# Column directions' input projections: u read in row order, PSUM written with steps

## The chip, the core and the metric

The kernel runs on one core of a Trainium2 chip, whose engines work side by side from queues of their own: TensorE (PE in the profile), VectorE (DVE), ScalarE (ACT), GpSimd (POOL) and the DMA queues, most of them issued by SyncE (SP). The time is the device time of one execution in microseconds (us), as the median of several executions. All data is fp32.

## What is computed

The reference is a network of two layers on a batch of 4 images with 384 channels and 32 x 32 positions (L = 1024). The first layer is a selective scan in four directions and a mixture of experts; the second is attention and an MLP. The change lies in the scan:

```
x0 = x.reshape(B, D, H * W)                              # row order
x1 = transpose(x, (0, 1, 3, 2)).reshape(B, D, H * W)     # column order
xs = stack([x0, x1, x0[..., ::-1], x1[..., ::-1]], 1)    # k = 0, 1, 2, 3
x_dbl = einsum('bkdl,kcd->bkcl', xs, x_proj_weight)      # 12 + 16 + 16 = 44 rows
dts, Bs, Cs = x_dbl[:, :, :12], x_dbl[:, :, 12:28], x_dbl[:, :, 28:]
dt = softplus(einsum('bkrl,kdr->bkdl', dts, dt_projs_weight) + bias)
h[l] = h[l-1] * exp(dt[l] * A) + dt[l] * u[l] * Bs[l]    # 16 states a channel
y[l] = sum over states of h[l] * Cs[l]
```

Directions 1 and 3 walk the image by columns. The einsum that makes x_dbl treats each position by itself, so its result does not depend on the order in which positions are taken, as long as each lands in its place.

## The kernel before

**Units.** `scan_layer` cuts the scan into 32 units: 4 batches, 4 directions in the order 0, 1, 3, 2, and 2 halves of 512 positions each. Directions 1 and 3 are called column units here (16 of the 32), 0 and 2 row units. u, the normalised input of a batch, stays in SBUF as 128 partitions x 3 chunks of channels x 1024 positions in row order: position (h, w) is element 32 h + w.

**Projection.** `project` (from L292) runs one unit ahead. It makes xd, 44 rows by 512 positions, with three matmuls into one PSUM bank, one for each chunk of channels (L316 to L319). `part(c)` (L302) gives the moving operand: for a row unit 512 contiguous elements of u, for a column unit the pattern "w, then h", in which neighbours lie 32 elements apart. `split` (L307) gives the bank in the shape w by h, which for a column unit is the contiguous bank in column order. ACT copies xd to SBUF (L321). Its B and C rows go to DRAM (L323) and come back, broadcast, as the tiles bcs (L329). The rest of xd is multiplied by the weights of dt (L344). ACT makes a softplus of it; DVE multiplies dt by u for the tile du (L382), with `part(c)` and `split` again; and both go to DRAM (L384, L385).

**Scan.** `chunk` (from L388) handles 128 channels of a unit. It reads dt and dt*u back (L403). For every group of states POOL multiplies dt*u by B into a tile bx (L419, 2 x 512 elements), ACT makes da = exp(dt*A) (L428), DVE scans along the positions (L433), and the product with C is made by DVE (L440) or POOL (L447). PE adds the states up with a selection matrix, into acc (L454). A bx tile is one of six (`bufs=6`): it is free when its acc matmuls are done. DVE adds acc into y (L281, L285). For a column unit it reads acc in PSUM with a step of 32 elements, so that y stays in row order.

**Order of the work.** A scheduler places all instructions at build time; each engine then takes its own in that fixed order. `next(project)` in `scan_layer` sets the xd block at the start of the unit before. From batch 1 on the tail of the batch before (`tail_batch`: routing, experts L906 to L925, attention L1030 to L1076, the last layers) is laid into the scan, and its matmuls stand in the same PE queue. After the last unit only tail work is left.

Of the kernel before, what the change touches and what calls it, by code (L numbers as in the profile page):

```python
# [20 lines left out]
DC = D // P  # L21
HW = 32
# [8 lines left out]
XD = R + 2 * NS  # L31
# [77 lines left out]
def halves(i):  # L109
    return slice(i * HF, (i + 1) * HF)  # L110


class Body:
# [68 lines left out]
    def scan_layer(self, x1, between):  # L182

        nc, tc, a = self.nc, self.tc, self.a
        with ExitStack() as ctx:
# [67 lines left out]
            for n, unit in enumerate(units):  # L253
# [3 lines left out]
                if n + 1 < len(units):  # L257
                    nb = units[n + 1][0]
                    if nb not in us:
                        us[nb] = start(nb)  # L260
                    project = self.project(units[n + 1], us[nb], wx, work, dram, psum, ahead)
                    next(project)
# [4 lines left out]
                for c in range(DC):  # L267
                    acc = psum.tile([P, HF], F32, tag="ps", name="acc")
                    for _ in self.chunk(
                        unit, n % NH == 0, c, fed, carry, nega, sel, acc, work, dap  # L270
                    ):
                        next(project, None)
                    if k % 2 == 0:
                        ys = y[:, c, halves(i)]
                        out = acc
                    else:
                        w = slice(i * (HW // NH), (i + 1) * (HW // NH))
                        ys = y[:, c, :].rearrange("p (h w) -> p h w", h=HW)[:, :, w]
                        out = acc.rearrange("p (w h) -> p h w", h=HW)
                    if k == 0:  # L280
                        nc.vector.scalar_tensor_tensor(  # L281
                            ys, us[b][:, c, halves(i)], dsum[:, c : c + 1], out, op0=ALU.mult, op1=ALU.add
                        )
                    else:
                        nc.vector.tensor_add(ys, ys, out)  # L285
# [6 lines left out]
    def project(self, unit, u, wx, work, dram, psum, made):  # L292

        nc, a = self.nc, self.a
        b, k, i = unit
        by_cols = k % 2 == 1
        w = slice(i * (HW // NH), (i + 1) * (HW // NH))  # L300

        def part(c):  # L302
            if by_cols:
                return u[:, c, :].rearrange("p (h w) -> p w h", h=HW)[:, w, :]
            return u[:, c, halves(i)]

        def split(ap):  # L307
            return ap.rearrange("p (w h) -> p w h", h=HW) if by_cols else ap

        def k2(name, shape=(P, HF)):  # L310
            return work.tile([*shape], F32, tag="k2", name=name, bufs=6)

        wdt = k2("wdt", (R, D))
        nc.sync.dma_start(out=wdt, in_=a["wdt"][:, k, :])
        ps = psum.tile([P, HF], F32, tag="ps", name="xd_ps")
        for c in range(DC):  # L316
            nc.tensor.matmul(
                split(ps[:XD, :]), wx[:, c, k, :], part(c), start=(c == 0), stop=(c == DC - 1)
            )  # L319
        xd = k2("xd", (XD, HF))  # L320
        nc.scalar.copy(xd, ps[:XD, :])  # L321
        rows = dram.tile([2 * NS, HF], F32, tag="rows", name="rows")
        nc.sync.dma_start(out=rows, in_=xd[R:XD, :])  # L323
        view = rows.rearrange("(t g n) l -> n t g l", t=2, g=NG)
        bcs = []
        for g in range(NG):
            bc = work.tile([P, 2, HF], F32, tag="bcs", name="bcs", bufs=5)
            for n in range(NJ):
                nc.sync.dma_start(  # L329
                    out=bc[n * DB : (n + 1) * DB], in_=view[n, :, g].partition_broadcast(DB)  # L330
                )
            bcs.append(bc)

        dd = dram.tile([2, D, HF], F32, tag="dd", name="dd")
        made += [bcs, dd]
        yield  # L340

        def begin(c):
            ps = psum.tile([P, HF], F32, tag="ps", name="dt_ps")
            nc.tensor.matmul(ps, wdt[:, c * P : (c + 1) * P], xd[:R, :], start=True, stop=True)  # L344
            bias = self.col("dtb", k * DC + c)
            mag, one_e, lnw = k2("mag"), k2("one_e"), k2("lnw")
            relu = k2("relu") if b == 0 else ps
            nc.scalar.activation(mag, ps, AF.Abs, bias=bias)
            nc.scalar.activation(relu, ps, AF.Relu, bias=bias)
            nc.scalar.activation(mag, mag, AF.Exp, scale=-1.0)  # L350
            nc.scalar.activation(one_e, mag, AF.Identity, bias=1.0)
            nc.scalar.activation(lnw, one_e, AF.Ln)
            if b == 0:
                nc.scalar.activation(one_e, one_e, AF.Identity, bias=1.0, scale=-1.0)
                terms = [lnw, one_e, mag, relu]
                for t in terms:
                    nc.tensor.matmul(
                        ps, self.ident, t, start=(t is terms[0]), stop=(t is terms[-1])
                    )
            else:  # L360
                nc.scalar.activation(one_e, one_e, AF.Identity, bias=self.minus1)
            return ps, mag, one_e, lnw

        def behind(engine):
            if self.place_behind is None:
                return nullcontext()
            return self.tc.issue_after(self.place_behind[engine])

        for c in range(DC):
            ps, mag, one_e, lnw = begin(c)  # L370
            yield
            if b > 0:
                with behind("pool"):
                    nc.gpsimd.tensor_sub(mag, one_e, mag)
                    nc.gpsimd.tensor_sub(lnw, lnw, mag)
            yield
            d, du = mag, one_e
            rows = slice(c * P, (c + 1) * P)
            with behind("dve"):
                if b > 0:  # L380
                    nc.vector.tensor_add(ps, ps, lnw)
                nc.vector.tensor_mul(split(du), split(ps), part(c))  # L382
            nc.scalar.copy(d, ps)  # L383
            nc.sync.dma_start(out=dd[0, rows, :], in_=d)  # L384
            ins = nc.sync.dma_start(out=dd[1, rows, :], in_=du).ins  # L385
        made.append(ins)
# [602 lines left out]
    def attention(self, xc, sums, room):  # L989
# [68 lines left out]

        steps = [(t, i, j) for t in range(HEADS // 2) for i in range(NH) for j in range(MB)]
        made = [project(0)]  # L1060
        ahead = scores(0, made[0][0], 0, 0, None)
        atts = []
# [366 lines left out]
```

## Time and profile before

| what | us |
|---|---|
| median of 3 executions | 4361.97 |
| lowest and highest | 4361.64 and 4367.63 |
| the profiled execution | 4365.25 |
| its span, first to last instruction | 4363.5 |
| of the span: PE busy | 3382.3 |
| POOL busy | 3049.6 |
| DVE busy | 2919.3 |
| ACT busy | 2504.0 |

The profile is of one execution. Its page gives busy sums, the span in 40 slices of 109 us (a digit is the busy share in tenths, PEclk the clock that TensorE was granted, in tenths of full speed), and groups of equal instructions with count, busy time, mean length, and the idle time of the engine ahead of them with what ended most of it. Other views of the trace are used too: one source line's instructions, busy sums in windows of time, and the timeline, in which neighbours of one kind are merged. Matmuls overlap: the next one starts before the one before has ended, so what a matmul costs PE is the distance of two starts and not its length.

### The profile page before, as it was taken

Reading aid. Unit: us, or ns where it says so; the run is one execution under the profiler, and the core shown is the slowest. Engines: PE = TensorE matmul, PEld = TensorE weight load, DVE = VectorE, ACT = ScalarE, POOL = GpSimd, SP = SyncE. Lnnn points to the kernel's source line nnn. Section 1 sums busy time; section 2 is a strip of 40 time slices with the busy share of each in tenths; the row PEclk is TensorE's granted clock in tenths of the full one; section 3 lists DMA queues with packets and bytes.
Section 4 is the critical chain, followed back from the end, with each engine's and each line's share of the span. In section 5 each row is a group of like instructions: output and inputs, shape, how many; then the busy total and the mean of one; then the engine's idle time right before and its main releaser. Section 6 shows DMA issues by size and latency. Waiting matters only on the chain. (4 is left out here: it accounts for less than half of the span.)

```text
span 4363.5 us, 46084 instructions
## 1 busy us (share of the span) xinstructions
PE 3382.3 (78%) x13436; PEld 1581.3 (36%) x13436; DVE 2919.3 (67%) x4331; ACT 2504.0 (57%) x4470; POOL 3049.6 (70%) x1475
## 2 busy tenths in 40 slices
PE   6545544379997895579997888579998799999896
PEld 2111111145553221235554322135554234666323
DVE  5888888967877868968787867968887740200102
ACT  4445545556665875466575777466666564343353
POOL 5999998898988968688898978789898831000100
PEclk7766776589997997779998999679999899999997
DMA  5444354577886534457779534457789434336200
GB/s 136 114 122 116 106 162 115 151 228 214 231 241 183 142 109 139 125 174 213 213 229 279 154 95 132 115 158 225 215 233 273 134 108 142 116 126 214 63 17 15
DMA packets 404756, 684.74 MB, mean 157 GB/s; under 512 B 50960, under 2 KB 206480, under 8 KB 404496
## 3 DMA queue, kind: packets, MB, share of 16 engines
q1 hardware_dynamic: 395184, 655.37, 51.9%
q0 software_dynamic: 8192, 25.17, 1.7%
q8 instruction: 108, 1.77, 0.2%
q14 instruction: 152, 1.25, 0.1%
q10 hardware_dynamic: 1120, 1.18, 0.1%
HBM read 561.47 MB, written 120.06 MB: 156 GB/s over the span
## 5 line engine op out<-in xcount | busy, mean ns | idle before, releaser
L419 POOL TENSOR_TENSOR bx<-dtr,bcs 128x1024 f32<-128x1024 f32 x768 | 1792.4, 2361 | 229.6 <-PE acc L454 118.7
L428 ACT ACTIVATE da<-dtr,nega 128x512 f32<-128x512 f32 x1536 | 1045.3, 690 | 945.8 <-DVE bx L440 564.3
L447 POOL TENSOR_TENSOR bx<-bx,bcs 128x1024 f32<-128x1024 f32 x384 | 903.1, 2359 | 179.1 <-DVE carry L444 74.3
L906 PE MATMUL h_ps<-xc,w 128*128 128x256 f32 (+1 forms) x3168 | 675.0, 368 | 60.8 <-DMA w<-in_w 18.7
L454 PE MATMUL acc<-bx,sel 128*32 128x512 f32 x3072 | 496.8, 697 | 289.2 <-POOL bx L447 232.4
L921 PE MATMUL y_ps<-w,hs 128*128 128x384 f32 x1824 | 643.2, 505 | 38.1 <-ACT hs L914 37.8
L906 PEld LDWEIGHTS h_ps<-xc,w 128*128 128x128 f32 x3168 | 556.1, 200 | 238.7 <-issue 112.8
L433 DVE TENSOR_TENSOR_SCAN bx<-da,carry,bx 128x512 f32<-128x512 f32 x384 | 474.7, 1270 | 129.3 <-ACT da L428 65.8
L433 DVE TENSOR_TENSOR_SCAN bx<-da,bx 128x512 f32<-128x512 f32 x384 | 453.3, 1210 | 117.1 <-POOL bx L419 59.2
L433 DVE TENSOR_TENSOR_SCAN da<-da,carry,bx 128x512 f32<-128x512 f32 x384 | 478.0, 1274 | 66.5 <-ACT da L428 60.9
L440 DVE TENSOR_TENSOR bx<-da,bcs 128x512 f32<-128x512 f32 x768 | 510.3, 680 | 3.7
L433 DVE TENSOR_TENSOR_SCAN da<-da,bx 128x512 f32<-128x512 f32 x384 | 456.2, 1219 | 63.3 <-ACT da L428 53.0
L921 PEld LDWEIGHTS y_ps<-w,hs 128*128 128x128 f32 x1824 | 350.0, 196 | 325.8 <-issue 78.2
L1036 ACT ACTIVATE ex<-s_ps 128x512 f32<-128x512 f32 x512 | 300.8, 592 | 156.6 <-PE s_ps L1030 154.4
L1030 PE MATMUL s_ps<-w 64*128 64x512 f32 x1024 | 307.9, 662 | 53.1 <-ACT ex L1036 51.8
L911 ACT ACTIVATE hs<-h_ps,bb 128x256 f32<-128x256 f32 (+1 forms) x528 | 201.0, 441 | 218.8 <-PE h_ps L906 218.4
L1076 PE MATMUL o_acc<-ex,vt 128*64 128x512 f32 x1024 | 287.0, 638 | 18.1 <-ACT ex L1036 11.5
L454 PEld LDWEIGHTS acc<-bx,sel 128*32 128x32 f32 x3072 | 80.0, 116 | 585.9 <-POOL bx L447 319.8
L942 POOL TENSOR_TENSOR diag<-ident,g_weight 128x1024 f32<-128x1024 f32 x8 | 15.0, 1893 | 345.6 <-PE xc_ps L889 331.0
L925 DVE TENSOR_TENSOR y<-y_ps,bb 128x384 f32<-128x384 f32 x76 | 41.7, 549 | 273.4 <-PE y_ps L921 273.4
L344 PE MATMUL dt_ps<-xd,wdt 12*128 12x512 f32 x192 | 123.2, 726 | 71.4 <-ACT mag L383 43.8
L1030 PEld LDWEIGHTS s_ps<-w 64*128 64x128 f32 x1024 | 82.8, 190 | 256.0 <-ACT ex L1036 206.0
(214 smaller groups left out, 3767.2 us busy)
## 6 DMA issues: line engine op xcount, KB each, us to landing
w<-in_w SPq DMA_DIRECT2D x352, 576.0 KB
dtr<-dd SPq DMA_DIRECT2D x1536, 128.0 KB
bcs<-rows SPq DMA_DIRECT2D x512, 128.0 KB
dd<-one_e SPq DMA_DIRECT2D x96, 256.0 KB
dd<-mag SPq DMA_DIRECT2D x96, 256.0 KB
rows<-zero SPq DMA_DIRECT2D x76, 192.0 KB
xs<-rows SPq DMA_DIRECT2D x32, 384.0 KB
made<-y SPq DMA_DIRECT2D x32, 384.0 KB
```

What stands on the lines that cost most here:

```text
L419: pool = nc.gpsimd.tensor_mul(bx, dtr[q][1], bc[:, 0].unsqueeze(1).to_broadcast([P, 2, HF])).ins
L428: nc.scalar.activation(da, dtr[q][0][:, j, :], AF.Exp, scale=nega[:, col : col + 1])
L433: nc.vector.tensor_tensor_scan(run(h), run(da), run(bx[:, j, :]), 0.0 if first else hold, ALU.mult, ALU.add,)
L440: dve = nc.vector.tensor_mul(bx[:, j, :], h, cg).ins
L447: pool = nc.gpsimd.tensor_mul(bx, bx, cg.unsqueeze(1).to_broadcast([P, 2, HF])).ins
L454: nc.tensor.matmul(acc[lo : lo + DB, :], sel, out[q][:, j, :], start=(g == 0), stop=(g == NG - 1),)
L906: nc.tensor.matmul(ps[:, r, :], w1[(f + r) // wf][:, c, (f + r) % wf * P : ((f + r) % wf + 1) * P], xc[:, c, :], start=(c == 0), stop=(c = ...
L911: nc.scalar.activation(hs[:, f + r, :], ps[:, r, :], AF.Identity, bias=bb[:, f + r : f + r + 1])
L921: nc.tensor.matmul(out[:, :D], hs[:, f, t * P : (t + 1) * P], w2[f // wf][:, f % wf, :], start=(f == 0), stop=(f == FC - 1),)
L1030: ins = nc.tensor.matmul(ps, w[rows, j * P : (j + 1) * P], w[rows, halves(i)], start=True, stop=True).ins
L1036: done.append(nc.scalar.activation(ex[:, o, :], ps, AF.Exp, scale=HD**-0.5, accum_out=sums[:, t, 2 * j + o, i : i + 1],).ins)
L1076: ins = nc.tensor.matmul(out[cols, :], made[t][1][:, j, cols], ex[:, o, :], start=(j == 0), stop=(j == MB - 1),).ins
```

## The change

For a column unit, the three xd matmuls read u in row order: for each of the 32 rows h, the 16 contiguous elements that belong to this half of the columns. The result is still kept in column order, so the PSUM side takes the steps: the bank is written in the shape h by w, where neighbours (w, w+1) lie 32 elements apart. Row units keep their patterns. L382 keeps `part` and `split`. The shapes and the sums stay; only the order in which a matmul takes its 512 positions changes. Eight lines are added, so line numbers after this place are 8 higher in the changed kernel: the matmul of L317 is L325 there.

```
--- before.py
+++ after.py
@@ -299,6 +299,14 @@
         by_cols = k % 2 == 1
         w = slice(i * (HW // NH), (i + 1) * (HW // NH))
 
+        def rows_of(c):
+            if by_cols:
+                return u[:, c, :].rearrange("p (h w) -> p h w", h=HW)[:, :, w]
+            return u[:, c, halves(i)]
+
+        def to_rows(ap):
+            return ap.rearrange("p (w h) -> p h w", h=HW) if by_cols else ap
+
         def part(c):
             if by_cols:
                 return u[:, c, :].rearrange("p (h w) -> p w h", h=HW)[:, w, :]
@@ -315,7 +323,7 @@
         ps = psum.tile([P, HF], F32, tag="ps", name="xd_ps")
         for c in range(DC):
             nc.tensor.matmul(
-                split(ps[:XD, :]), wx[:, c, k, :], part(c), start=(c == 0), stop=(c == DC - 1)
+                to_rows(ps[:XD, :]), wx[:, c, k, :], rows_of(c), start=(c == 0), stop=(c == DC - 1)
             )
         xd = k2("xd", (XD, HF))
         nc.scalar.copy(xd, ps[:XD, :])
```

More of the change, by code (lines that the diff above doesn't have):

```diff
@@ L300, in project, with rows_of, to_rows @@
         w = slice(i * (HW // NH), (i + 1) * (HW // NH))
+        def rows_of(c):
+            if by_cols:
+                return u[:, c, :].rearrange("p (h w) -> p h w", h=HW)[:, :, w]
+            return u[:, c, halves(i)]
+        def to_rows(ap):
+            return ap.rearrange("p (w h) -> p h w", h=HW) if by_cols else ap
         def part(c):
@@ L317, in project @@
             nc.tensor.matmul(
-                split(ps[:XD, :]), wx[:, c, k, :], part(c), start=(c == 0), stop=(c == DC - 1)
+                to_rows(ps[:XD, :]), wx[:, c, k, :], rows_of(c), start=(c == 0), stop=(c == DC - 1)
             )
```

## The prediction

> **What bounds the kernel now.** I read the page's busy sums and 40 slices first, then the costliest groups.
>
> ```profile
> PE 3382.3 (78%) x13436; PEld 1581.3 (36%) x13436; DVE 2919.3 (67%) x4331; ACT 2504.0 (57%) x4470; POOL 3049.6 (70%) x1475
> PE   6545544379997895579997888579998799999896
> POOL 5999998898988968688898978789898831000100
> PEclk7766776589997997779998999679999899999997
> ...
> L419 POOL TENSOR_TENSOR bx<-dtr,bcs 128x1024 f32<-128x1024 f32 x768 | 1792.4, 2361 | 229.6 <-PE acc L454 118.7
> ```
>
> POOL leads the scan (31 slices): a unit needs 24 products of L419 and 12 of L447, 36 x 2.36 = 85.0 us, and a unit of batch 0 lasts 88 us (118 to 206 us). In batches 1 to 3 the expert, attention and MLP matmuls of the batch before share PE with the scan, and the windows by unit show PE as full as POOL:
>
> ```profile
> 206.00:294.00 88.00, 47.86 (x135) 11.24 (x134) 78.76 (x115) 44.87 (x70) 83.50 (x37) 0.69 0.44 115
> 1120.00:1231.00 111.00, 105.94 (x425) 61.94 (x424) 90.00 (x102) 68.32 (x108) 98.31 (x46) 0.97 0.76 213
> ```
>
> (Columns: window, its length, busy PE, weight load, DVE, ACT, POOL, clock, DMA.) In batch 0 a shorter PE job buys nothing; in the second window PE idles 5 us of 111.
>
> Next the changed line alone. An fp32 matmul leaves two records, so a unit's three leave six.
>
> ```profile
> L317 PE MATMUL xd_ps<-u,wx x6: 1034/1035/1035, 1029.0 to 1033.2; 128*44 128x512 f32 x6
> ...
> L317 PE MATMUL xd_ps<-u,wx x6: 592/592/627, 1586.0 to 1588.2; 128*44 128x512 f32 x6
> ...
> L317 PE MATMUL xd_ps<-u,wx x6: 593/1061/1082, 789.2 to 793.5; 128*44 128x512 f32 x6
> ```
>
> First a column unit, then a row unit at full clock, then a row unit mostly at half clock. A record's length holds its latency; what it costs PE is the spacing of starts: (1033.2-1029.0)/5 = 0.84 us for columns, (1588.2-1586.0)/5 = 0.44 at full clock; at 0.1 us resolution. From the block's busy time, finer: (5.33-1.035)/5 = 0.859 us, and, with 2.77 us in the windows below, (2.77-0.592)/5 = 0.436, or 0.429 past the first start. So I use 858 and 429 ns: 512 columns at 1.68 and 0.84 ns. The column price stays near 858 at any clock; a contiguous record costs about 854 at half clock (1061-593 = 468 more, latency included).
>
> Last, one block in the timeline, with who stands behind it:
>
> ```profile
> 1120.23 5.33 PE L317 MATMUL xd_ps<-u,wx 128*44 128x512 f32 x6
> 1125.60 0.58 ACT L321 COPY xd<-xd_ps 44x512 f32<-44x512 f32 x1 [3.11 <-PE xd_ps L317]
> 1128.92 1.06 PE L454 MATMUL acc<-bx,sel 128*32 128x512 f32 x8
> 1130.07 4.67 POOL L419 TENSOR_TENSOR bx<-dtr,bcs 128x1024 f32<-128x1024 f32 x2 [3.19 <-PE acc L454]
> ```
>
> PE runs the block in its order, so the acc matmuls come later, their bx buffers come free later, and POOL stands 3.19 us. ACT stands too, with da (L428) behind the copy.
>
> [...] No matmul of before writes with steps, so this is untested, and it is the crux. [...]
>
> **The change part by part.** The instruction lists of the two programs are the same on every engine in number, order and waits, DMAs included; nothing is moved. Only the 16 column units' xd matmuls differ, 96 records.
>
> *Removed:* the stepped read. The new read takes runs of 16 fp32, 64 bytes[...]; I cost it as contiguous. Up to 858-429 = 429 ns a record at full clock, 2.57 us a unit; nothing at half clock. The granted clock in these windows (columns: window, length, PE, weight load, clock, DMA) sorts the units:
>
> ```profile
> 1028.90:1034.30 5.40, 5.33 (x6) 0.70 (x6) 1.00 0.59 225
> ...
> 1836.50:1842.00 5.50, 5.36 (x6) 0.92 (x6) 0.56 0.03 7
> ...
> 2746.60:2752.00 5.40, 5.36 (x6) 0.92 (x6) 0.50 0.28 100
> ...
> 3189.90:3192.80 2.90, 2.77 (x6) 0.64 (x6) 1.00 1.04 282
> ```
>
> The last is a row unit. Of the 12 column units of batches 1 to 3, ten stand at 1.00; the two at 0.56 and 0.50 do not, and I count them at nothing. PE saves 10 x 2.57 = 25.7 us there.
>
> *Added:* PSUM writes at a step of 32 fp32, three passes accumulating. Bounds: 0.84 ns a column (free), 1.68 (as SBUF), 3.35 (twice that). The nearest rows are DVE's, on the same two steps:
>
> ```profile
> L382 DVE TENSOR_TENSOR one_e<-dt_ps,u x3: 989/1001/1028, 256.7 to 290.2; 128x512 f32<-128x512 f32 x3
> L285 DVE TENSOR_TENSOR y<-y,acc x2: 665/676/687, 269.2 to 292.4; 128x512 f32<-128x512 f32 x2
> ...
> L382 DVE TENSOR_TENSOR one_e<-dt_ps,u x3: 677/681/691, 605.3 to 638.9; 128x512 f32<-128x512 f32 x3
> L285 DVE TENSOR_TENSOR y<-y,acc x3: 678/689/689, 577.4 to 639.5; 128x512 f32<-128x512 f32 x3
> ```
>
> The first pair is a column unit, the second a row unit. Reading u with steps costs DVE 320 ns; reading acc in PSUM at the very step the change writes costs nothing[...]. [...] I take free. It is a read, not an accumulating write: hence the two rivals.
>
> *How much reaches the end.* In batch 0 the four blocks lie beside POOL's products (83.5 of 88 us busy), which start at their own pace from full buffers; I take 0. Were that cover gone, the three blocks there at a clock of 0.92 to 1.00 would give 3 x 2.57 = 7.7 us. ACT's copy of xd and the DMAs of rows and bcs behind it come up to 2.57 us earlier, for a unit that starts 88 us or more later: 0. In batches 1 to 3 I count POOL's stalls right behind each block, capped by what the block gives up (2.57, or 1.72 where an acc group sits after the fourth record). By start time: 913.0: 1.50; 1120.2: 2.57 (stall 3.19); 1231.1: 1.72 (1.79); 1953.4: 1.26; 2067.2: 2.57 (2.85); 2884.3: 2.50; 3102.6: 1.05; at 1029.0, 2156.6 and 2976.2 none. The stalls at 913.0, 1231.1 and 2884.3 stand as "issue", but POOL starts just as an acc group ends. Sum 13.2 us, half of PE's 25.7. Some will be lost (late next: DVE's scans, for which POOL waits at L447), some gained where PE is short and POOL does not show it; I leave 13.2.
>
> The profiled execution took 4365.25 us (span 4363.5, 1.75 around it): 4352.1. It lay 3.3 above the median of 4361.97, so the forecast is 4361.97-13.2 = **4349**.
>
> **Rivals.**
> 1. *PSUM's step costs what SBUF's did*, 1.68 ns a column: records stay at 858, time **4362**. For: [...]SBUF's behaviour. Against: L285.
> 2. *Slower: the accumulating write needs over 1.68 ns[...].* The place is the same block; it decides from 858 ns a record. At 1287 PE gains 12 x 2.57 = 31 us, half reaches POOL: 4378. At 1717 it is 62 us, some 42 reach POOL as buffers run dry, and in batch 0 ACT, which already stands 2.7 to 3.7 us at three of the four blocks, delays DVE (79 of 88 us busy) by some 2 us each: +50, **4412**. [...] Against: L285 again, and reads and writes of contiguous sums that keep pace at 429.
> 3. *Writes are free but the time is given back*: POOL's next stall, on DVE or a DMA, swallows it. In 913 to 1325 us POOL waits 19 us for DVE, 14 for DMA and 12 for PE. Some 4 us are left: **4358**.
>
> **How the numbers follow.** Forecast 0.44, rival 1 0.18, rival 2 0.24, rival 3 0.14. The likeliest case alone spans 4336 (all of 25.7) to 4353. The range, 4336 to 4380, takes in rivals 1 and 3 and the mild end of 2, leaving out some 0.18: 0.03 under 4336, and 0.15 of rival 2 from a record of about 1350 ns on. About 0.2% (8.7 us) is what a measurement here can tell from no change: faster 0.44, same 0.33 (rivals 1 and 3, less 0.01, and 0.02 of rival 2's weakest form), slower 0.23.
>
> **What would show it.** Free: column records of L325 at 592 ns at full clock, blocks of 2.77 us instead of 5.33, POOL's stall at the block near 1120 us under 1 us. Rival 1: records at 1035. Rival 2: over 1035. Rival 3: 592, and POOL idle moved from PE to DVE or DMA. I am wrong if the run-lengths of 16 cost reads of their own, or if the time moves though the records do not.

## The result and the profile after

The changed kernel takes 4345.85 us (median of 8 executions) against 4362.18 us (8 executions of the kernel before): ratio 0.9962, interval 0.9951 to 0.9973, or 16.6 us less (11.8 to 21.4). The forecast was 4349, 13.2 us less. The profiled execution took 4349.06 us, with a span of 4347.3.

The page's busy sums and slices after the change:

```profile
PE 3336.8 (77%) x13436; PEld 1575.1 (36%) x13436; DVE 2919.5 (67%) x4331; ACT 2504.3 (58%) x4470; POOL 3049.9 (70%) x1475
...
PE   6545544379997884579897887579997899998896
...
POOL 5999998898989978689898978789888830000100
PEclk8666666589998997789998998779999899999997
...
L427 POOL TENSOR_TENSOR bx<-dtr,bcs 128x1024 f32<-128x1024 f32 x768 | 1793.5, 2364 | 217.0 <-PE acc L462 116.0
```

PE's busy time fell by 45.5 us; the other engines' stayed within 0.4. So the change took work from PE alone; the other engines do the same work and only wait less. Of the 45.5 us, the 16 column blocks themselves give about 35 (from 85.9 to 51.0, the time under at least one record of L317 or L325). The rest is about what two executions of one kernel differ by: a second trace of the kernel before has 3373.0 us of PE, 9.3 less than the first.

The changed line itself, in the column unit shown before (now at 1019.9 us) and in a row unit:

```profile
L325 PE MATMUL xd_ps<-u,wx x6: 592/592/627, 1019.9 to 1022.1; 128*44 128x512 f32 x6
...
L325 PE MATMUL xd_ps<-u,wx x6: 593/593/627, 2612.1 to 2614.2; 128*44 128x512 f32 x6
```

They are the same, 592 and 593 ns a record at the median: the stepped PSUM write costs a column unit nothing that can be seen here. Windows on the same line (columns: window, length, PE, weight load, clock, DMA share, GB/s) show the block near 1111 us and the two at a low clock:

```profile
1110.90:1113.80 2.90, 2.77 (x6) 0.64 (x6) 1.00 1.05 226
1820.00:1826.00 6.00, 5.11 (x6) 1.01 (x6) 0.57 0.12 32
2726.00:2731.00 5.00, 4.23 (x6) 0.93 (x6) 0.63 0.30 108
```

2.77 us as forecast; in the window at a clock of 0.57 the block still takes 5.11 us, in the one at 0.63 it takes 4.23. Both took 5.36 before.

The timeline at the block near 1111 us:

```profile
1110.96 2.77 PE L325 MATMUL xd_ps<-u,wx 128*44 128x512 f32 x6
...
1113.77 0.58 ACT L329 COPY xd<-xd_ps 44x512 f32<-44x512 f32 x1 [0.56 <-PE xd_ps L325]
...
1117.10 1.06 PE L462 MATMUL acc<-bx,sel 128*32 128x512 f32 x8
...
1118.24 6.99 POOL L427 TENSOR_TENSOR bx<-dtr,bcs 128x1024 f32<-128x1024 f32 x3 [0.62 <-PE acc L462]
```

ACT's wait for xd went from 3.11 us to 0.56, POOL's wait for acc from 3.19 to 0.62. The latter is the full 2.57 us that this block was to give.

POOL's waits in a stretch where PE is nearly full, from the first product of unit 9 to that of unit 13 (the same work in both; 904.7 to 1331.6 us before, 898.6 to 1315.4 after; columns: us in total, times, longest). Before:

```profile
POOL bx L447 <- DVE carry L444: 11.8, 6, 4.3
POOL bx L419 <- PE acc L454: 11.7, 5, 4.8
POOL bx L419 <- DMA dtr<-dd: 11.4, 4, 5.4
...
POOL bx L419 <- issue: 3.3, 2, 1.8
...
```

After:

```profile
POOL bx L455 <- DVE carry L452: 12.4, 5, 4.3
...
POOL bx L427 <- DMA dtr<-dd: 7.5, 2, 5.1
POOL bx L427 <- PE acc L462: 6.6, 4, 3.4
POOL bx L427 <- issue: 2.7, 1, 2.7
...
```

The wait for acc fell by 5.1 us and "issue" (idle time for which the profile shows no wait) by 0.6, which are the stalls that the forecast had counted here (1.50, 2.57 and 1.72). The wait for a DMA fell by 3.9, which it had not counted. That is scatter: a second trace of the kernel before has 8.0 us of it in this stretch, 3.4 less than the first, without any change. The waits for DVE did not fall.

### The profile page after: what moved, and what is told of

It is laid out like the page before. It is cut to its first block, busy times and chain, and to the rows that moved or that the text cites. A ratio compares the mean times of both kernels' runs of the same rounds, so it can differ in the third digit from the quotient of the medians.

```text
span 4347.3 us, 46084 instructions
## 1 busy us (share of the span) xinstructions
PE 3336.8 (77%) x13436; PEld 1575.1 (36%) x13436; DVE 2919.5 (67%) x4331; ACT 2504.3 (58%) x4470; POOL 3049.9 (70%) x1475
## 3 DMA queue, kind: packets, MB, share of 16 engines
q8 instruction: 108, 1.77, 0.2%
## 5 line engine op out<-in xcount | busy, mean ns | idle before, releaser
L1084 PE MATMUL o_acc<-ex,vt 128*64 128x512 f32 x1024 | 283.3, 630 | 19.1 <-ACT ex L1044 11.8
L933 DVE TENSOR_TENSOR y<-y_ps,bb 128x384 f32<-128x384 f32 x76 | 41.6, 548 | 264.3 <-PE y_ps L929 264.2
```

The costliest lines, as they stand in the source:

```text
L1084: ins = nc.tensor.matmul(out[cols, :], made[t][1][:, j, cols], ex[:, o, :], start=(j == 0), stop=(j == MB - 1),).ins
```

## The experiments

Where the gain arises is read from one mark, the start of the first POOL product of a unit. Stage lengths between marks, us, one profiled execution each:

| kernel | start to unit 0 | unit 0 to 9 | unit 9 to 13 | unit 13 to 30 | unit 30 to end |
|---|---|---|---|---|---|
| before | 43.8 | 860.9 | 426.9 | 1958.3 | 1073.6 |
| before_again | 43.6 | 860.7 | 426.2 | 1952.1 | 1073.8 |
| after | 41.1 | 857.5 | 416.8 | 1951.7 | 1080.2 |
| after_again | 41.6 | 857.7 | 420.7 | 1951.0 | 1073.7 |
| acc_step | 43.7 | 857.8 | 432.8 | 1966.7 | 1069.8 |
| b0_only | 43.9 | 856.6 | 423.7 | 1968.5 | 1083.7 |
| b123_only | 41.1 | 861.1 | 417.0 | 1958.3 | 1086.9 |
| rows_step | 44.6 | 861.2 | 418.5 | 1976.4 | 1086.0 |
| du_rows | 41.9 | 854.4 | 419.4 | 1969.0 | 1084.2 |

The last four ran on another chip, where the kernel before takes 4384.16 us; their last stage is some 10 us longer, so their ratios, which are against the kernel before on that chip, are what counts. The first column ends before any column block: it differs by 3 us between kernels that are the same up to there.

**The two kernels again.** No edit; the second execution of each shows the noise.

> The changed kernel once more, on the chip of the others. 0.9962 of the kernel before by its first runs; with the interval 0.995 to 0.998. In its trace the gain from the first product of unit 9 to that of unit 13 should again be 8 to 12 us against the kernel before.

> The kernel before, for a second trace on the chip of the others: it shows how far two executions of one kernel lie apart at the same marks. Expected: the first product of every unit within 3 us of the first trace up to unit 13; if more, the part of the gain that was placed by unit is noise.

Measured: 0.9962 again (0.9947 to 0.9976), median 4345.21. The gain from unit 9 to 13 is 6.2 us in this trace and 10.1 in the first, against 8 to 12 expected. The second trace of the kernel before keeps within 1.1 us of the first up to unit 13, then drifts, to 7.3 us at unit 24. Other pairs lie further apart: from unit 9 to 13 the two traces of the changed kernel differ by 3.9 us, and b0_only, which changes nothing there, is 2.5 to 3.2 us under the kernel before. Taken together, the three traces without the new pattern in that stage (before, before_again, b0_only) have 423.7 to 426.9 us and the five with it and no slowed acc groups 416.8 to 420.7, so the gain there is about 7 us. The gain by stage between 13 and 30, 0.4 to 7.3 us according to the pair, can't be read.

**b0_only and b123_only: one part of the change each.**

```
-                to_rows(ps[:XD, :]), wx[:, c, k, :], rows_of(c), ...
+                (to_rows if b == 0 else split)(ps[:XD, :]), wx[:, c, k, :], (rows_of if b == 0 else part)(c), ...
```

and the same with `b > 0`.

> The new pattern only in batch 0 (4 of the 16 column units). Theory (POOL covers those blocks, the gain is PE time that POOL waits for in batches 1 to 3): 0 to 3 us under the kernel before, which has 4362. Rival (ACT's stall on the copy of xd, 2.7 to 3.7 us a block, feeds DVE, which is 79 of 88 us busy): most of 4 x 2.6 = 10 us, about 4353.

> The new pattern only in batches 1 to 3 (12 column units). Theory: 10 to 13 us under the kernel before, so 4349 to 4352, with about 10 of it between the first products of units 9 and 13, where PE is full. Rival (batch 0 carries it): under 5 us, over 4357.

Measured: b0_only 0.9991 (0.9978 to 1.0004), or 3.9 us less than 4384, not told apart from none. b123_only 0.9969 (0.9960 to 0.9978): 13.6 us less. They add up to 17.5, the whole being 16.6. Batch 0's part shows better in the stage from unit 0 to 9: 856.6 to 857.8 us in the four traces with the new pattern there and nothing else changed in that stage but acc_step's groups, 860.7 to 861.1 in the three without. It is 3 to 4 us, not 0.

The stalls that the forecast had counted one by one can be followed in the traces, since POOL has the same products in the same order in every kernel. POOL's idle time ahead of the seven products, us; the columns are the starts of the xd blocks in the kernel before:

| | 913.0 | 1120.2 | 1231.1 | 1953.4 | 2067.2 | 2884.3 | 3102.6 |
|---|---|---|---|---|---|---|---|
| forecast to go | 1.50 | 2.57 | 1.72 | 1.26 | 2.57 | 2.50 | 1.05 |
| before | 1.50 | 3.19 | 1.79 | 1.26 | 2.85 | 2.50 | 1.05 |
| before_again | 1.51 | 3.17 | 1.77 | 1.26 | 2.99 | 2.49 | 1.05 |
| b0_only | 1.51 | 3.19 | 1.79 | 1.27 | 3.35 | 2.49 | 1.05 |
| after | 0.00 | 0.62 | 0.06 | 0.00 | 0.00 | 0.00 | 0.00 |
| after_again | 0.00 | 0.62 | 0.08 | 0.00 | 0.03 | 0.00 | 0.00 |
| b123_only | 0.00 | 0.13 | 0.00 | 0.00 | 0.48 | 0.00 | 0.00 |
| acc_step | 1.78 | 3.50 | 4.28 | 0.04 | 1.69 | 1.40 | 0.00 |

One pair as the timelines have it, the product behind the block at 2067.2 us, before and after:

```profile
2077.63 4.67 POOL L419 TENSOR_TENSOR bx<-dtr,bcs 128x1024 f32<-128x1024 f32 x2 [2.85 <-PE acc L454]
...
2058.61 4.69 POOL L427 TENSOR_TENSOR bx<-dtr,bcs 128x1024 f32<-128x1024 f32 x2
```

All seven go or nearly go, 13.5 us in all from before to after against 13.2 forecast, and they do so in after, after_again and b123_only, while all stand in before, before_again and b0_only. acc_step, described next, brings five of them back. An eighth wait, 0.7 to 1.0 us behind the block at 2746.6 us, goes as well, but there the next product of L447 then waits 1.2 us for DVE instead of 0.1 to 0.5.

**acc_step: PE time given back, but not through xd.**

```
-                    nc.tensor.matmul(
-                        acc[lo : lo + DB, :], sel, out[q][:, j, :],
-                        start=(g == 0), stop=(g == NG - 1),
-                    )
+                    slow = c == DC - 1 and g > 0 and k < 2
+                    step = lambda ap: ap.rearrange("p (a s) -> p s a", s=HW) if slow else ap
+                    nc.tensor.matmul(step(acc[lo : lo + DB, :]), sel, step(out[q][:, j, :]), start=(g == 0), stop=(g == NG - 1))
```

> The changed kernel, and three acc groups near each of the 16 xd blocks read bx and write PSUM at a step of 32, so that about as much PE time comes back as the change took away (0.86 us a group, 2.6 a unit), but xd itself and ACT's copy of it stay early. If the gain runs through PE's order to acc, bx and POOL: batch 0 keeps its 3 to 4 us (up to the first product of unit 9), batches 1 to 3 lose theirs, the time is 10 to 13 over the changed kernel. If it runs through ACT, which no longer stands before the copy: the gain stays everywhere, within 4 us of the changed kernel.

Measured: 1.0025 of the kernel before (1.0016 to 1.0034), so 26 to 27 us over the changed kernel (1.0063 of it). A slowed group cost more than I had set. Two of them in the timeline, PE alone:

```profile
1223.35 2.59 PE L464 MATMUL acc<-bx,sel 128*32 128x512 f32 x8
...
1236.53 2.48 PE L464 MATMUL acc<-bx,sel 128*32 128x512 f32 x8
```

They take 2.48 to 2.59 us instead of 1.06: 1.46 us a group from its first start to the next matmul's (median 2.46 against 1.00). Not all of them add as much: at half clock a contiguous group takes about 1.93 us already (the one at 152.36 us in the kernel before, at a clock of 0.50), and most of these groups of batch 0 run at half clock in the changed kernel (their records have a median of 1060 ns from 130 to 900 us). Counted by their records, the slowed groups add 47.6 us in batches 1 to 3, where the blocks had given 26.9, and 6.1 in batch 0, where the blocks had given 8.1. PE's sums from unit 0 to 9, which the clock moves too, are (window, length, PE, weight load, DVE, ACT, POOL, clock, DMA share, GB/s; before, after, acc_step):

```profile
43.80:904.70 860.90, 431.79 (x1276) 118.27 (x1277) 740.11 (x1060) 437.26 (x687) 782.87 (x356) 0.68 0.48 132
...
41.10:898.60 857.50, 417.53 (x1277) 115.79 (x1277) 739.79 (x1060) 437.35 (x687) 782.66 (x357) 0.67 0.49 133
...
43.70:901.50 857.80, 423.63 (x1275) 116.38 (x1275) 740.08 (x1060) 437.80 (x688) 783.86 (x357) 0.69 0.49 133
```

The two theories part by batch. From unit 9 to 13 the stage turns from 416.8 or 420.7 us to 432.8, over the kernel before, although xd stays early, and stalls of POOL come back (the table above). So in batches 1 to 3 what counts is PE time at these places, also when acc groups take it. The exchange rate agrees too: 26 to 27 us for 47.6 of PE here, 13.6 for 26.9 in b123_only, about half in both. Unit 0 to 9 keeps the whole gain (857.8 us), although PE works 6.1 us more there. So in batch 0, where PE idles about half the time, PE time is not what counts; what is left is when xd is done.

Batch 0's path is seen at the block of unit 3. The timeline before, ACT, DVE and POOL behind the block:

```profile
211.83 0.58 ACT L321 COPY xd<-xd_ps 44x512 f32<-44x512 f32 x1 [3.18 <-PE xd_ps L317]
...
213.10 2.46 DVE L433 TENSOR_TENSOR_SCAN bx<-da,carry,bx 128x512 f32<-128x512 f32 x2 [1.65 <-ACT da L428]
...
219.32 2.46 DVE L433 TENSOR_TENSOR_SCAN bx<-da,carry,bx 128x512 f32<-128x512 f32 x2 [0.23 <-ACT da L428]
...
221.93 2.35 POOL L447 TENSOR_TENSOR bx<-bx,bcs 128x1024 f32<-128x1024 f32 x1 [0.85 <-DMA dtr<-dd]
```

After:

```profile
206.75 0.58 ACT L329 COPY xd<-xd_ps 44x512 f32<-44x512 f32 x1 [0.62 <-PE xd_ps L325]
...
209.17 2.46 DVE L441 TENSOR_TENSOR_SCAN bx<-da,carry,bx 128x512 f32<-128x512 f32 x2 [0.23 <-ACT da L436]
...
215.39 2.46 DVE L441 TENSOR_TENSOR_SCAN bx<-da,carry,bx 128x512 f32<-128x512 f32 x2 [0.23 <-ACT da L436]
...
216.18 4.66 POOL L455 TENSOR_TENSOR bx<-bx,bcs 128x1024 f32<-128x1024 f32 x2
```

ACT stood 3.18 us before the copy, with da queued behind it; DVE then stood 1.65 us for da, and its next pair of scans was late as well; and POOL lost 0.85 us two products later. The label of that wait says DMA, but the product reads bx of the scans that began at 219.32 us, and these ended at 221.78, just before it started. After the change the scans end at 217.85, before POOL comes to the product, and the idle time is gone.

Four such waits of POOL lie behind the blocks of units 3 and 4: 0.85, 0.46, 1.02 and 0.30 us. All four are there in the three traces of that comparison without the new pattern in batch 0, and none in the four with it, acc_step included. That is 2.6 of the 3 to 4 us; the rest was not placed. Behind the block of unit 2 ACT had not stood at all; behind that of unit 5 it had stood 2.67 us, and no wait of POOL goes with it. From first product to first product, units 1 to 3 are 1.0, 1.1 and 1.2 us shorter.

**probe: the disputed cost by itself.** Ahead of the scan, 16 groups of 24 accumulating 128x512 matmuls:

```
+        for name, w, x in (("pf", self.ident, xf), ("pb", wb, xb)):      # fp32, bf16
+            for step in (1, 2, 4, 32):
+                run(f"{name}_write_" + called[step], w, x, 1, step)
+            for step in (2, 4, 8, 32):
+                run(f"{name}_read_" + called[step], w, x, step, 1)
```

> The changed kernel with 16 groups of 24 accumulating 128x512 matmuls ahead of the scan, which cost time of their own and whose sums go nowhere: fp32 and bf16, with the PSUM write or the SBUF read at a step of 2, 4, 8 or 32 elements and the other side contiguous. Distance of starts at full clock. Theory[...]: fp32 records 429 ns for every write step; reads 429 at step 2, 858 from step 4 on; bf16 216 contiguous, 429 for every write step, reads 216 up to step 4 and 858 from step 8 on. Rival (PSUM writes don't care for steps): bf16 writes 216 throughout. Rival ([...]the xd case is lucky): fp32 writes over 429 at some step.

Measured, median distance of starts in ns (fp32: per record). The clock was 1.00 but for the last two bf16 reads, at 0.58 for step 8 and 0.50 for step 32:

| step | fp32 write | fp32 read | bf16 write | bf16 read |
|---|---|---|---|---|
| 1 | 429 | 429 | 216 | 216 |
| 2 | 429 | 449 | 429 | 226 |
| 4 | 429 | 900 | 429 | 451 |
| 8 | not run | 920 | not run | 900 |
| 32 | 429 | 860 | 429 | 857 |

The groups in the trace (name, count, busy us, mean ns of one):

```profile
L314 PE MATMUL pf_read_far<-p_xf,ident 128*128 128x512 f32 x48 | 41.5, 1037 | 0.0
...
L314 PE MATMUL pf_write_one<-p_xf,ident 128*128 128x512 f32 x48 | 20.8, 592 | 0.0
...
L314 PE MATMUL pf_write_far<-p_xf,ident 128*128 128x512 f32 x48 | 20.8, 592 | 0.0
...
L314 PE MATMUL pb_write_far<-p_both 128*128 128x512 bf16 x24 | 10.5, 634 | 0.0
...
L314 PE MATMUL pb_write_one<-p_both 128*128 128x512 bf16 x24 | 5.4, 380 | 0.0
```

48 records at any write step take 20.8 us in fp32, while a read at a step of 32 doubles them (41.5); in bf16 a stepped write doubles the group (10.5 us against 5.4). Stepped writes start 429 ns apart in both types, 0.84 ns for each of 512 columns, and fp32 takes those 429 ns without steps too. Both rivals are out. The prices expected for bf16 and for steps of 2 to 8 were the author's estimates. The large miss is the bf16 read at step 4, 451 instead of 216; the other reads lie within 8% of what was expected.

**rows_step: the row units stepped on both sides.**

```
-            return u[:, c, halves(i)]
+            return u[:, c, halves(i)].rearrange("p (h w) -> p w h", w=HW)
...
-            return ap.rearrange("p (w h) -> p h w", h=HW) if by_cols else ap
+            return ap.rearrange("p (w h) -> p h w", h=HW) if by_cols else ap.rearrange("p (h w) -> p w h", w=HW)
```

> The changed kernel, and the row units now also take their positions in steps of 32 elements on both sides, reading u and writing PSUM (the same sums in another order of positions). If the read's step alone costs and the write's is free beside it: row records at 1035 ns, as column records were, PE plus 2.57 us in every row unit at full clock, and half of that at the end: 10 such units in batches 1 to 3, some 13 us over the changed kernel, about 4359. If the two steps add up: records over 1035 ns (1460 for twice the added time), and about 4372.

A row unit's block in its trace:

```profile
L325 PE MATMUL xd_ps<-u,wx x6: 1037/1037/1037, 1582.8 to 1587.1; 128*44 128x512 f32 x6
```

The steps don't add up: 1037 ns, the price of the read alone (1035 for columns before). The time is 1.0018 of the kernel before (1.0009 to 1.0027), about 24 us over the changed kernel instead of 13. The row blocks' records take 35.6 us more of PE than in the changed kernel (10.9 in the blocks of units 0 to 9, 24.7 behind them), so about two thirds reach the end; with the intervals of both times, half is at the edge of what fits. Part of it is batch 0: unit 0 to 9 goes from 857.5 to 861.2 us, though the new column pattern is in this kernel too. Whether the row blocks' share is truly larger, and why, was not settled; their places in the queues are others.

**du_rows: the same pattern for VectorE.** In PSUM, DVE's stepped read (676 ns at L285 against 689) and the matmul's stepped write (592 ns a record against 593) cost nothing. A stepped write of du in SBUF might be as cheap, and would spare DVE's stepped read of u:

```
-                nc.vector.tensor_mul(split(du), split(ps), part(c))
+                nc.vector.tensor_mul(to_rows(du), to_rows(ps), rows_of(c))
```

> The changed kernel, and VectorE's dt*u of the column units also goes in row order: u in runs of 16, dt read in PSUM and du written in SBUF at a step of 32. If a stepped SBUF write is as free as a stepped PSUM access: 680 ns instead of 1043, 48 of them, VectorE minus 17 us, of which a third to a half reaches the end: 4338 to 4341. If the stepped write costs what the stepped read did: 1043 ns and 4346, no change against the changed kernel.

A column unit of batch 0, then a row unit:

```profile
L390 DVE TENSOR_TENSOR one_e<-dt_ps,u x3: 1020/1021/1039, 251.7 to 285.1; 128x512 f32<-128x512 f32 x3
...
L390 DVE TENSOR_TENSOR one_e<-dt_ps,u x3: 682/682/692, 597.2 to 630.7; 128x512 f32<-128x512 f32 x3
```

The stepped write to SBUF costs DVE what the stepped read did, 1021 ns at the median against 1001. The runs of 16 are not the cause: L285 reads and writes y in such runs for a column unit and takes 676 ns there (lines in the prediction). The time is 0.9955 of the kernel before (0.9940 to 0.9969), no different from the changed kernel's 0.9962, though its one trace is 3 us shorter up to unit 9. No version here beats the changed kernel.

## Why the prediction was right, step by step

- *The record's price, 858 to 429 ns.* Right: starts lie 429 ns apart, a record of 1035 ns became one of 592, a block of 5.33 us one of 2.77.
- *The stepped PSUM write at nothing.* Right: in probe stepped writes start 429 ns apart in both types, 0.84 ns a column. For fp32 that is what writes without steps take (429 throughout); for bf16 it doubles the time (216 to 429). What pointed to it beforehand was DVE's read of acc at that step (676 ns against 689 at L285), at about 1.02 ns an element (an estimate from the trace before: 549 ns for 384 elements at L925 and 680 for 512 at L440), which is near a matmul's 0.84. That a matmul's write would keep pace as this read does was the author's estimate; no trace of before showed it.
- *No gain at half clock.* Right at 0.57: contiguous records start 853 to 854 ns apart there, and the block takes 5.11 us against 5.36. At 0.63 the block gave 1.1 us, since the clock rose within it, from 0.50 up to 2729 us to 1.00 from 2730 us on: its last starts are 626 and 430 ns apart.
- *Batch 0 at nothing.* Wrong in size: 3 to 4 us. The step went by POOL's busy share. It knew that ACT stands before the copy with da behind it, and rival 2 even priced that path, at some 2 us a block for DVE, should the block get longer; but the forecast took the same path at nothing for a block that gets shorter. Two of the waits that it cost POOL, 0.85 and 1.02 us, carried the label of a DMA. acc_step supports this: with 6.1 us of PE time returned, but xd early, batch 0 keeps its gain and these waits stay away.
- *POOL's stalls behind the blocks, 13.2 us.* Right, stall by stall: the seven that were counted shrink by 13.5 us in the first trace, and b123_only gives 13.6 (9.6 to 17.5). By stage the forecast had 5.8 us for units 9 to 13, where about 7 are measured; its 7.4 for units 13 to 30 can't be read from stage lengths, only from the stalls.
- *Rival 3, the time given back.* Not borne out to unit 30. In the first trace the last stage is 6.6 us longer than before, in the second it is equal (1073.7 against 1073.6), so that is the scatter of executions.
- *The sum.* 13.2 forecast, 16.6 (11.8 to 21.4) measured; batch 0's 3 to 4 us are about the difference, though the interval alone would allow for none.

## What to carry to other kernels

When a matmul has to reorder its columns, measure the step on each side by itself: for fp32 the PSUM write was free (429 ns a record at every step), and the SBUF read was what doubled the time (860 to 920 ns at steps of 4 to 32). For bf16 the write doubled it too (429 against 216). To price an idle queue, follow every engine that waits for the block, not only the fullest one: here ACT's wait before the copy cost batch 0 three to four us, part of which the labels of POOL's waits gave to a DMA. And what PE time is worth depends on its place: little where PE idles half the time, about half of it in batches 1 to 3, where PE is full for long stretches (400.6 of 426.9 us from unit 9 to 13).

## What the runs showed of the hardware that was not expected

An fp32 read at steps of 4 and 8 elements (900 and 920 ns) is slightly slower than at 32 (860), and step 2 costs 449, not 429. A bf16 read slows at step 4 already (451 against 216). By the distance of neighbours in bytes the two types agree: at 8 bytes 449 (fp32) and 451 (bf16), at 16 bytes 900 and 900, and further apart no more than a little above that (fp32 920 at 32 bytes and 860 at 128, bf16 857 at 64). So neighbours 8 bytes apart cost fp32 nearly nothing (449 against 429) and double bf16 (451 against 216). The access pattern with steps on both sides costs what the read alone does (1037 ns a record in rows_step, 1035 for the read alone). DVE pays for a stepped SBUF write as for a stepped read (1021 and 1001 ns at the median in the same unit, against 682 unstepped), and nothing for a stepped PSUM read (676 against 689 at L285).
